# A local-attention transformer on one core: the order of work inside one pipelined step

## Chip, cores and metric

The kernel runs on one core of a Trainium2 chip. Times are device microseconds of one execution. Five engines run their own queues of instructions in order: TensorE (PE, with its weight loads PEld), VectorE (DVE), ScalarE (ACT), GpSimd (POOL) and SyncE (SP), which here only issues DMAs. They wait for one another through semaphores.

## The reference

The input is x, 16 sequences of 256 tokens with 128 channels. Two adaptive layer-norm blocks follow each other. The first has a linear attention and then a six-layer local transformer; the second a causal attention with a position bias and a feed-forward net. The change touches the local transformer alone. Its six layers are, in the reference's words (lines joined and cut):

```python
def attn_layer(x, Wqkv, qs, ksc, Wo):            # 16 heads of 64 channels
    q, k, v = jnp.split(x @ Wqkv, 3, -1)
    q = l2norm(q) * qs;  k = l2norm(k) * ksc
    q = q * cos * scale + rotate_half(q) * sin * scale
    k = k * cos * inv + rotate_half(k) * sin * inv
    out = local_attention(q, k, v)               # windows of 32 queries, 64 keys, softmax
    return out @ Wo
def ffn_layer(x, g, bln, W1, b1, W2, b2):
    hg = layernorm(x) * g + bln;  a, gate = jnp.split(hg @ W1 + b1, 2, -1)
    return a * gelu(gate) @ W2 + b2
for i in range(6):
    x = attn_layer(shift_tokens(x), ...) + x
    x = ffn_layer(shift_tokens(x), ...) + x
```

## The kernel before

All of it is float32, channels on partitions. The 16 sequences form eight units of two sequences (512 tokens). The state of a unit stays on chip as a tile z.

The local transformer is one software-pipelined loop (lines 1002 to 1079) over N = 192 positions: 6 layers x 8 units x 4 steps. A step n starts two head pairs (four of the 16 heads) of a unit, and does later stages of work that began in earlier steps. Inside the block, TensorE, DVE, ScalarE and POOL keep the order in which the source issues instructions (`manual_schedule`, line 991), so the order of the calls in the loop body is the order of each engine's queue. SP is not in that list.

The stages of one pair of steps, with the engines that they use:

- `project` (635): two matmuls per head pair (query and key, line 647) into two PSUM banks; DVE makes from each bank a rotated part `sent` (648) and a straight part (651); ScalarE squares the bank (653). Four DMAs on SP swap halves of `sent` into `got`.
- `rotate` (660): one step later POOL adds `got` to the query and key, four operations of line 662 per step.
- `norms_sum` (665), `norms_inverse` (682), `norms_rows` (719): in every second step the squares of four pairs are summed per head on TensorE (670) and copied by ScalarE to n2 (679), transposed (688), turned to inverse square roots by DVE (690, 699) and eleven small POOL operations (706 to 714), and one step later sent as rows by DMA. `widened` and `scaled` bring the key's factors back and multiply them in on POOL (743).
- `masked` (764) and `scores` (780): four steps after the projection the mask goes into two PSUM tiles `sim`, one for each head of a pair ("par"), and small matmuls (791) add the scores of both pairs ("x").
- `maxima` (800): DVE takes row maxima (803) and makes the Exp's bias nb (805).
- `exponentials` (808): ScalarE runs 16 Exp of 128x64 (812), each followed by a read of its row sum.
- `divided` (821): DVE's reciprocal (823) of all 16 sums and one POOL product (825) over 128x1024.
- `flipped` (829): in the next step TensorE transposes pr (834) into two banks, which ScalarE (842) and DVE (840) copy to prT.
- `windows`, `weighted` (844), `merging` (870): value windows are transposed (753), multiplied by the probabilities (852), copied to zx by ScalarE and DVE (867, 865), and merged with the value-output weights (873) into y. After four steps DVE adds y to the state (886).
- `ffn` (894): the feed-forward of a unit is a generator of ten pieces. `go_on(behind)` is called three times per step and runs one piece at each call. The generator starts at the third call of the step with n = 0 modulo 4 (mean 899, subtraction 901, square 903). At n = 1 the first call does the variance and POOL's power and spreading (917, 919), the third the transposes (924), 925 and 926. At n = 2 the first call does the gates (932, 934), the second the three GELUs (939). At n = 3 the first call does 944 and 948, the third the last matmuls (955) and the addition to the state (888).

PSUM has eight banks: four for the tag "mm" (all products named mm in the profile), three for `sim`, one for y. A tile of "mm" waits until an earlier one has been read for the last time.

The order inside a step before: `scaled`, `rotate`; merging and the addition to the state; norm rows; first `go_on(behind)`; windows; flip; mask; `weighted`; second `go_on`; in even steps the norm sums; scores, maxima, 16 Exp; in even steps the inverse norms; first pair's `project`; third `go_on`; second pair's `project`; `divided`; the row DMAs. ScalarE's queue thus has all 16 Exp ahead of the squares of both pairs.

Of the kernel before, what the change touches and what calls it, by code (L numbers as in the profile page):

```python
# [14 lines left out]
ALU = mybir.AluOpType  # L15
# [29 lines left out]
def adaln_kernel(  # L45
# [5 lines left out]
    nc = tc.nc  # L51
# [27 lines left out]
    def small(tag, shape, bufs=4):  # L79
        return sm.tile(list(shape), F32, tag=tag, name=tag, bufs=bufs)  # L80
# [469 lines left out]
    with ExitStack() as es:  # L550
# [84 lines left out]
        def project(i, u, m, wqk):  # L635


            xs = zs[u][:, :, PAD : PAD + L]
            squares = []
            sent, got = atile("sent", (128, 2, 512)), atile("got", (128, 2, 512))  # L640
            q = two(atile("q", (128, 512), 8))
            k = ks[m % 8][:, :, PAD:]
            for j, (name, r) in enumerate((("q", q), ("k", k))):
                tab = [rope[:, j, a].unsqueeze(1).to_broadcast([128, 2, L]) for a in range(2)]
                scale = bcol(i, name + "s")
                pp = bank()
                nc.tensor.matmul(pp, wqk[:, j, :], xs, start=True, stop=True)  # L647
# [5 lines left out]
                nc.scalar.activation(sq, pp, AF.Square)  # L653
                squares.append(sq)
            for c in range(0, 128, 64):
                nc.sync.dma_start(got[c : c + 32], sent[c + 32 : c + 64])
                nc.sync.dma_start(got[c + 32 : c + 64], sent[c : c + 32])
            return q, squares, got

        def rotate(m, q, got):  # L660
            for j, r in enumerate((q, ks[m % 8][:, :, PAD:])):
                nc.gpsimd.tensor_tensor(r, r, two(got[:, j, :]), ALU.add)  # L662


        def norms_sum(squares):
# [12 lines left out]
            n2 = work("n2")  # L678
            nc.scalar.copy(n2, pn)
            return n2  # L680
# [59 lines left out]
        def scaled(m, kn):  # L740

            k = ks[m % 8][:, :, PAD:]
            nc.gpsimd.tensor_tensor(k, k, two(kn), ALU.mult)  # L743
# [61 lines left out]
            nc.vector.scalar_tensor_tensor(nb, mx, -1.0, rn, ALU.mult, ALU.mult)  # L805
            return nb

        def exponentials(par, sim, nb, rn, pr, ssum):
            for x in range(2):
                for st in range(4):  # L810
                    b = 4 * x + st
                    nc.scalar.activation(  # L812
                        pr[:, x, st, par, :],
                        sim[:, b * 64 : (b + 1) * 64],
                        AF.Exp,
                        bias=nb[:, b : b + 1],
                        scale=rn[:, b : b + 1],
                        accum_out=ssum[:, x, st, par : par + 1],
                    )

        def divided(pr, ssum):
            rsum = small("rsum", (128, 16))
            nc.vector.reciprocal(rsum, ssum.rearrange("p x t h -> p (x t h)"))  # L823
            prf = pr.rearrange("p x t h k -> p (x t h) k")
            nc.gpsimd.tensor_tensor(  # L825
                prf, prf, rsum.unsqueeze(2).to_broadcast([128, 16, 64]), ALU.mult
            )

        def flipped(p, pr, prT):
# [137 lines left out]
        N = DEPTH * per  # L967
        wqk = [load_qk(0, p) for p in range(NP)]
        wff = load_ffn(0)
        vos = {}  # L970
        qs, squares, got, prs, prTs = {}, {}, {}, {}, {}
        xws, zxs, pys = {}, {}, {}
        inverses, kns = {}, {}
        n2 = rk = home = None
        behind, merges = [], []

        def place(n):

            return n // per, n % per // QS, 2 * (n % QS)
# [21 lines left out]
        n = 0  # L1001
        while n < N + 9 or behind:
            layer, at_ = divmod(n, per)
            if at_ == 12 and 0 < layer < DEPTH:
                wff = load_ffn(layer)

            if 0 <= n - 4 < N:
                for x in range(2):
                    scaled(2 * (n - 4) + x, kns.pop(2 * (n - 4) + x))
            if 0 <= n - 1 < N:  # L1010
                for x in range(2):
                    m = 2 * (n - 1) + x
                    rotate(m, qs[m], got.pop(m))

            w, j = divmod(n - 9, QS)
            if 0 <= w < DEPTH * NU:
                if j == 0:
                    pys[w] = psy.tile([128, 512], F32, tag="y", name="y")
                merging(j, zxs.pop((w, j)), vos[w // NU], pys[w])
                if j == QS - 1:  # L1020
                    add_to_state(w % NU, pys.pop(w))
            if n % 2 and 3 <= n <= N + 1:
                home = norms_rows(rk)
            go_on(behind)
            go_on(merges)
            for s, lag in ((0, 7), (1, 9)):
                v, r = divmod(n - lag, QS)
                if r == 0 and 0 <= v < DEPTH * NU:
                    xws[v, s] = windows(v % NU, s)
            if 0 <= n - 5 < N:  # L1030
                i, u, p = place(n - 5)
                if p == 0:
                    prTs[i, u] = atile("prT", (128, NP, 512))
                flipped(p, prs.pop(n - 5), prTs[i, u])
            sims = masked() if 0 <= n - 4 < N else None

            v, r = divmod(n - 8, QS)
            if 0 <= v < DEPTH * NU:
                zxs[v, r] = weighted(r, xws[v, r // 2], prTs[v // NU, v % NU])
            go_on(behind)  # L1040
            if n % 2 == 0 and 2 <= n <= N:
                n2 = norms_sum([squares.pop(m) for m in range(2 * n - 4, 2 * n)])
            if sims:
                m = 2 * (n - 4)
                rn = inverses[m // 4][:, m % 4 // 2]
                scores(sims, m, [qs.pop(m), qs.pop(m + 1)])
                pr = atile("pr", (128, 2, 4, 2, 64), 1)
                ssum = small("ssum", (128, 2, 4, 2))
# [51 lines left out]
    with ExitStack() as es:  # L1100
# [23 lines left out]
        for p in range(NP):  # L1124
            bias = wc.tile([128, 2, 384], F32, tag=f"bias{p}", name=f"bias{p}")
# [176 lines left out]
        N = len(steps)  # L1302
# [3 lines left out]
        qs, prs, prTs, oTs, pys, running, merging = {}, {}, {}, {}, {}, [], []  # L1306
        n = 0
# [147 lines left out]
```

## Time and profile before

| | |
|---|---|
| median of 3 runs | 4600.04 us (4599.63 to 4603.97) |
| the profiled execution's own time | 4603.96 us |
| its span, first to last instruction | 4602.2 us |
| mean granted TensorE clock | 0.966 of full speed |
| busy: PE, PEld | 4075.4 us (89%), 2645.1 us (57%) |
| busy: DVE, ACT, POOL | 2730.6 (59%), 2932.2 (64%), 2572.2 us (56%) |
| busy PE in 440 to 3900 us, the local transformer | 3123.3 of 3460 us, clock 0.99 |

The time of an instruction group, and the idle time of its engine just before it with what ended that idle time, stand in one line of the profile: "busy, mean ns of one | idle us <-releaser". A row of the timeline gives the start and the time taken in us, the engine, the line, the operation and the tiles; a bracket at its end gives the idle time before it. A matmul of float32 shows as two records. Matmuls overlap, so their times do not add up exactly.

### The profile page before, as it was taken

Reading aid. Unit: us, or ns where it says so; the run is one execution under the profiler, and the core shown is the slowest. Engines: PE = TensorE matmul, PEld = TensorE weight load, DVE = VectorE, ACT = ScalarE, POOL = GpSimd, SP = SyncE. Lnnn points to the kernel's source line nnn. Section 1 sums busy time; section 2 is a strip of 40 time slices with the busy share of each in tenths; the row PEclk is TensorE's granted clock in tenths of the full one; section 3 lists DMA queues with packets and bytes.
Section 4 is the critical chain, followed back from the end, with each engine's and each line's share of the span. In section 5 each row is a group of like instructions: output and inputs, shape, how many; then the busy total and the mean of one; then the engine's idle time right before and its main releaser. Section 6 shows DMA issues by size and latency. Waiting matters only on the chain.

```text
span 4602.2 us, 119189 instructions
## 1 busy us (share of the span) xinstructions
PE 4075.4 (89%) x45721; PEld 2645.1 (57%) x45721; DVE 2730.6 (59%) x5795; ACT 2932.2 (64%) x9846; POOL 2572.2 (56%) x3110
## 2 busy tenths in 40 slices
PE   6677799999999989999999999999999998899998
PEld 4443566666666666666666666666665666545454
DVE  3434666666666666666666666666666665455554
ACT  2333666766666676666666666666767666377776
POOL 3323666666666666666666666666665665144332
PEclk8678899999999999999999999999999999899999
DMA  1023444344444344444344344343434432200000
GB/s 30 5 35 91 106 99 100 97 104 100 98 102 103 96 100 102 102 99 102 96 100 105 95 104 100 100 100 94 107 98 100 100 92 73 66 3 3 6 3 8
DMA packets 193553, 371.11 MB, mean 81 GB/s; under 512 B 42537, under 2 KB 83416, under 8 KB 192984
## 3 DMA queue, kind: packets, MB, share of 16 engines
q1 hardware_dynamic: 192984, 363.50, 32.3%
q8 instruction: 361, 5.91, 0.5%
q14 instruction: 208, 1.70, 0.1%
HBM read 127.92 MB, written 8.91 MB: 30 GB/s over the span
## 4 chain that ended last, share of the span: by engine, by line
PE 55%; DVE 19%; ACT 10%; issue 4%; POOL 1%; DMA 0%; DVEq 0%; SPq 0%; POOLq 0%; ACTq 0%
PE y L873 11%; PE mm L852 8%; PE mm L647 6%; PE sim L791 5%; DVE sent L648 5%; PE mm L834 3%; PE mm L944 3%; DVE mx L803 3%; PE mm L932 3%; ACT pr L812 2%; PE mm L955 2%; DVE k L651 2%; PE mm L670 2%; DVE q L651 2%; ACT fg L939 2%
## 5 line engine op out<-in xcount | busy, mean ns | idle before, releaser
L812 ACT ACTIVATE pr<-sim,nb,rq 128x64 f32<-128x64 f32 x3072 | 1190.9, 429 | 283.0 <-DVE nb L805 213.5
L647 PE MATMUL mm<-z,wqk 128*128 128x512 f32 x1536 | 764.0, 611 | 161.2 <-DVE fx L901 63.6
L825 POOL TENSOR_TENSOR pr<-pr,rsum 128x1024 f32<-128x1024 f32 x192 | 365.0, 1901 | 921.9 <-DVE rsum L823 914.1
L873 PEld LDWEIGHTS y<-zx,wvo 128*128 128x128 f32 x6144 | 723.2, 193 | 92.5 <-issue 90.5
L873 PE MATMUL y<-zx,wvo 128*128 128x128 f32 x6144 | 724.4, 277 | 0.8 <-ACT zx L867 0.7
L812 ACT ACTIVATION_READ_ACCUMULATOR pr<-sim,nb,rq 128x1 f32 x3072 | 707.7, 230 | 0.0
L648 DVE SCALAR_TENSOR_TENSOR sent<-mm,vec,rope 128x512 f32<-128x512 f32 x768 | 572.0, 745 | 36.9 <-PE mm L647 28.5
L647 PEld LDWEIGHTS mm<-z,wqk 128*128 128x128 f32 x1536 | 263.6, 191 | 474.2 <-issue 154.2
L662 POOL TENSOR_TENSOR q<-q,got 128x512 f32<-128x512 f32 x384 | 488.2, 1271 | 11.1 <-DMA got<-sent 10.8
L743 POOL TENSOR_TENSOR k<-k,kn 128x512 f32<-128x512 f32 x384 | 480.2, 1271 | 15.7 <-DMA kn<-rkh 15.6
L662 POOL TENSOR_TENSOR k<-k,got 128x512 f32<-128x512 f32 x384 | 488.7, 1273 | 0.0
L803 DVE TENSOR_REDUCE mx<-sim 128x8 f32<-128x512 f32 x384 | 263.8, 687 | 329.2 <-PE sim L791 329.2
L653 ACT ACTIVATE sq<-mm 128x512 f32<-128x512 f32 x768 | 422.8, 672 | 36.9 <-DVE q L651 24.3
L867 ACT COPY zx<-mm 128x512 f32<-128x512 f32 x384 | 224.9, 586 | 347.5 <-PE mm L852 347.5
L852 PE MATMUL mm<-prT,xw 64*128 64x256 f32 x3072 | 391.0, 393 | 24.9 <-DVE prT L840 24.8
L865 DVE COPY zx<-mm 128x512 f32<-128x512 f32 x384 | 265.5, 691 | 227.2 <-PE mm L852 227.2
L1215 POOL TENSOR_TENSOR pr<-pr,rsum 128x256 f32<-128x256 f32 (+1 forms) x256 | 206.1, 826 | 317.6 <-DVE rsum L1213 310.2
L852 PEld LDWEIGHTS mm<-prT,xw 64*128 64x128 f32 x3072 | 294.7, 189 | 131.0 <-ACT prT L842 104.2
L791 PEld LDWEIGHTS sim<-k,q 64*32 64x32 f32 x24576 | 264.9, 105 | 120.8 <-issue 111.3
L791 PE MATMUL sim<-k,q 64*32 64x64 f32 x24576 | 297.7, 226 | 6.4 <-POOL k L743 5.1
L840 DVE COPY prT<-mm 128x512 f32<-128x512 f32 x192 | 132.8, 692 | 270.4 <-PE mm L834 269.2
L1204 ACT ACTIVATE pr<-lg,nm 128x128 f32<-128x128 f32 (+1 forms) x512 | 226.5, 444 | 93.3 <-DVE nm L1193 81.4
(237 smaller groups left out, 6664.1 us busy)
## 6 DMA issues: line engine op xcount, KB each, us to landing
got<-sent SPq DMA_DIRECT2D x1536, 128.0 KB
kn<-rkh SPq DMA_DIRECT2D x768, 128.0 KB
xw<-xw SPq DMA_DIRECT2D x96, 256.0 KB
wqk<-in_L_ffn_Wqkv_dram SPq DMA_DIRECT2D x48, 128.0 KB
bhome<-brow SPq DMA_DIRECT2D x1, 3072.0 KB
wv<-in_L_ffn_Wqkv_dram SPq DMA_DIRECT2D x12, 256.0 KB
wo<-in_L_ffn_Wo_dram SPq DMA_DIRECT2D x12, 256.0 KB
xt<-in_x_dram SPq DMA_DIRECT2D x8, 256.0 KB
```

Source lines behind the costliest of these rows:

```text
L647: nc.tensor.matmul(pp, wqk[:, j, :], xs, start=True, stop=True)
L648: nc.vector.scalar_tensor_tensor(two(sent[:, j, :]), two(pp), scale, tab[1], ALU.mult, ALU.mult)
L653: nc.scalar.activation(sq, pp, AF.Square)
L662: nc.gpsimd.tensor_tensor(r, r, two(got[:, j, :]), ALU.add)
L743: nc.gpsimd.tensor_tensor(k, k, two(kn), ALU.mult)
L791: nc.tensor.matmul(sims[par][32 * c : 32 * c + 32, c0 : c0 + 64], q[r, s, t0 : t0 + 32], k[r, s, t0 : t0 + 64], start=False, stop=True, sk ...
L803: nc.vector.tensor_reduce(mx, sim.rearrange("p (b k) -> p b k", b=8), AX.X, ALU.max)
L812: nc.scalar.activation(pr[:, x, st, par, :], sim[:, b * 64 : (b + 1) * 64], AF.Exp, bias=nb[:, b : b + 1], scale=rn[:, b : b + 1], accum_o ...
L825: nc.gpsimd.tensor_tensor(prf, prf, rsum.unsqueeze(2).to_broadcast([128, 16, 64]), ALU.mult)
L852: nc.tensor.matmul(pz[par][:, w * 256 : (w + 1) * 256], xw[r, (2 * k + w) % 8, :], prT[r, :, 64 * k + 32 * w : 64 * k + 32 * w + 32], star ...
L865: nc.vector.tensor_copy(dst, src)
L873: nc.tensor.matmul(py[:, j * 128 : (j + 1) * 128], vo[:, h, :], zx[:, h % 2, h // 2, :], start=(h == 0), stop=(h == 2 * NP - 1), skip_grou ...
```

## The change

Four things move inside the loop body; no arithmetic on the data is added or removed.

1. The exponentials are done by head pair (x) rather than by head of a pair (par): eight Exp for the first pair, then the first pair's projection with its squares, then eight Exp for the second pair, then the second pair's projection. Sums, reciprocal and POOL product are made per pair: two reciprocals of 128x8 and two products of 128x512 take the place of one of 128x16 and one of 128x1024.
2. The third `go_on(behind)`, a feed-forward piece, runs ahead of both projections rather than between them.
3. The norm sums run ahead of `weighted` and of the second `go_on`, rather than after them.
4. `rotate` runs after the first `go_on(behind)` and `go_on(merges)`, rather than right after `scaled`.

```diff
-        def exponentials(par, sim, nb, rn, pr, ssum):
-            for x in range(2):
+        def exponentials(x, sims, nbs, rn, pr):
+
+            ssum = small("ssum", (128, 4, 2))
+            for par in range(2):
                 for st in range(4):
                     b = 4 * x + st
                     nc.scalar.activation(
                         pr[:, x, st, par, :],
-                        sim[:, b * 64 : (b + 1) * 64],
+                        sims[par][:, b * 64 : (b + 1) * 64],
                         AF.Exp,
-                        bias=nb[:, b : b + 1],
-                        scale=rn[:, b : b + 1],
-                        accum_out=ssum[:, x, st, par : par + 1],
+                        bias=nbs[par][:, b : b + 1],
+                        scale=rn[:, par, b : b + 1],
+                        accum_out=ssum[:, st, par : par + 1],
                     )
+            return ssum
 
         def divided(pr, ssum):
-            rsum = small("rsum", (128, 16))
+            rsum = small("rsum", (128, 8))
...
-                prf, prf, rsum.unsqueeze(2).to_broadcast([128, 16, 64]), ALU.mult
+                prf, prf, rsum.unsqueeze(2).to_broadcast([128, 8, 64]), ALU.mult
             )
...
-            if 0 <= n - 1 < N:
-                for x in range(2):
-                    m = 2 * (n - 1) + x
-                    rotate(m, qs[m], got.pop(m))
...
             go_on(behind)
             go_on(merges)
+            if 0 <= n - 1 < N:
+                for m in (2 * (n - 1), 2 * (n - 1) + 1):
+                    rotate(m, qs[m], got.pop(m))
...
+            if n % 2 == 0 and 2 <= n <= N:
+                n2 = norms_sum([squares.pop(m) for m in range(2 * n - 4, 2 * n)])
             v, r = divmod(n - 8, QS)
             if 0 <= v < DEPTH * NU:
                 zxs[v, r] = weighted(r, xws[v, r // 2], prTs[v // NU, v % NU])
             go_on(behind)
-            if n % 2 == 0 and 2 <= n <= N:
-                n2 = norms_sum([squares.pop(m) for m in range(2 * n - 4, 2 * n)])
             if sims:
...
                 nbs = [maxima(sims[par], rn[:, par]) for par in range(2)]
-                for par in range(2):
-                    exponentials(par, sims[par], nbs[par], rn[:, par], pr, ssum)
+                ssum = exponentials(0, sims, nbs, rn, pr)
...
-            if n < N:
-                i, u, p = place(n)
-                m = 2 * n
-                qs[m], squares[m], got[m] = project(i, u, m, wqk[p])
             if 0 <= w < DEPTH * NU and j == QS - 1:
                 behind.append(ffn(w % NU, w // NU, *wff))
             go_on(behind)
-            if n < N:
-                m = 2 * n + 1
-                qs[m], squares[m], got[m] = project(i, u, m, wqk[p + 1])
-            if sims:
-                divided(pr, ssum)
-                prs[n - 4] = pr
+            for x in range(2):
+                if n < N:
+                    i, u, p = place(n)
+                    m = 2 * n + x
+                    qs[m], squares[m], got[m] = project(i, u, m, wqk[p + x])
+                if sims:
+                    divided(pr[:, x], ssum)
+                    if x == 0:
+                        ssum = exponentials(1, sims, nbs, rn, pr)
+                    else:
+                        prs[n - 4] = pr
```

More of the change, by code (lines that the diff above doesn't have):

```diff
@@ L813, in exponentials @@
                         pr[:, x, st, par, :],
-                        sim[:, b * 64 : (b + 1) * 64],
+                        sims[par][:, b * 64 : (b + 1) * 64],
                         AF.Exp,
-                        bias=nb[:, b : b + 1],
-                        scale=rn[:, b : b + 1],
-                        accum_out=ssum[:, x, st, par : par + 1],
+                        bias=nbs[par][:, b : b + 1],
+                        scale=rn[:, par, b : b + 1],
+                        accum_out=ssum[:, st, par : par + 1],
                     )
+            return ssum
         def divided(pr, ssum):
-            rsum = small("rsum", (128, 16))
-            nc.vector.reciprocal(rsum, ssum.rearrange("p x t h -> p (x t h)"))
-            prf = pr.rearrange("p x t h k -> p (x t h) k")
+            rsum = small("rsum", (128, 8))
+            nc.vector.reciprocal(rsum, ssum.rearrange("p t h -> p (t h)"))
+            prf = pr.rearrange("p t h k -> p (t h) k")
             nc.gpsimd.tensor_tensor(
-                prf, prf, rsum.unsqueeze(2).to_broadcast([128, 16, 64]), ALU.mult
+                prf, prf, rsum.unsqueeze(2).to_broadcast([128, 8, 64]), ALU.mult
             )
@@ L1007, in adaln_kernel @@
             if 0 <= n - 4 < N:
-                for x in range(2):
-                    scaled(2 * (n - 4) + x, kns.pop(2 * (n - 4) + x))
-            if 0 <= n - 1 < N:
-                for x in range(2):
-                    m = 2 * (n - 1) + x
-                    rotate(m, qs[m], got.pop(m))
+                for m in (2 * (n - 4), 2 * (n - 4) + 1):
+                    scaled(m, kns.pop(m))
             w, j = divmod(n - 9, QS)
@@ L1047, in adaln_kernel @@
                 pr = atile("pr", (128, 2, 4, 2, 64), 1)
-                ssum = small("ssum", (128, 2, 4, 2))
                 nbs = [maxima(sims[par], rn[:, par]) for par in range(2)]
-                for par in range(2):
-                    exponentials(par, sims[par], nbs[par], rn[:, par], pr, ssum)
+                ssum = exponentials(0, sims, nbs, rn, pr)
             if n % 2 == 0 and 2 <= n <= N:
                 rk, inverses[n // 2 - 1] = norms_inverse(n2)
-            if n < N:
-                i, u, p = place(n)
-                m = 2 * n
-                qs[m], squares[m], got[m] = project(i, u, m, wqk[p])
             if 0 <= w < DEPTH * NU and j == QS - 1:
```

## The prediction

> **What bounds the kernel now.** I read the page first (busy shares, slices, chain that ended last), then the groups by line, then the timeline of single steps, engine by engine. The slices put about 3,500 of the 4,602 us into the local-attention loop, which is all that the diff touches (first Square of line 653 at 411.7 us, last Exp of line 812 at 3,926.8).
>
> ```profile
> PE 4075.4 (89%) x45721; PEld 2645.1 (57%) x45721; DVE 2730.6 (59%) x5795; ACT 2932.2 (64%) x9846; POOL 2572.2 (56%) x3110
> ...
> PE 55%; DVE 19%; ACT 10%; issue 4%; POOL 1%; DMA 0%; DVEq 0%; SPq 0%; POOLq 0%; ACTq 0%
> ```
>
> TensorE is busiest, but the chain leaves it for 45% of the span: it is paced by hand-backs. The groups name them.
>
> ```profile
> L647 PE MATMUL mm<-z,wqk 128*128 128x512 f32 x1536 | 764.0, 611 | 161.2 <-DVE fx L901 63.6 <-DVE fx L925 52.2 <-DVE z L888 37.9
> ...
> L852 PE MATMUL mm<-prT,xw 64*128 64x256 f32 x3072 | 391.0, 393 | 24.9 <-DVE prT L840 24.8
> ...
> L688 PE MATMUL mm<-ident,n 128*128 128x128 f32 x384 | 63.9, 288 | 51.6 <-ACT n L679 50.3 <-issue 1.2
> ...
> L924 PE MATMUL mm<-ident,fs 128*128 128x128 f32 x192 | 31.7, 288 | 29.2 <-POOL fs L919 29.2
> ...
> L722 PE MATMUL mm<-ident,rk 128*32 128x128 f32 x96 | 26.2, 273 | 40.3 <-ACT sq L653 34.2 <-POOL rk L713 6.1
> ```
>
> Each is one gap per four steps (a unit; 48 units). Sorting TensorE's idle time of 1800 to 2400 us by step number n modulo 4 gives, per unit: 1.45 us at n=0 (line 647 waits for 901) and 0.53 (852 for 840); 1.14 at n=1 (647 for 925) and 0.63 (924 for 919); 1.08 at n=2 (688 for 679) and 0.57 (722 for 653); 0.84 at n=3 (647 for 888) and 0.18 (834 for pr). Sum 6.42, times 48 = **308 us**, the most that reordering can win unless TensorE itself gets cheaper.
>
> Two stretches of the timeline show the mechanisms. The first is n=0, the second n=2.
>
> ```profile
> 2050.59 0.67 DVE L901 TENSOR_TENSOR fx<-z,mm 128x512 f32<-128x512 f32 x1
> ...
> 2051.32 1.12 PE L647 MATMUL mm<-z,wqk 128*128 128x512 f32 x2 [1.45 <-DVE fx L901]
> ```
>
> ```profile
> 2006.61 1.28 ACT L939 ACT_TABLE_LOAD   x1
> ...
> 2007.90 1.95 ACT L939 ACTIVATE fg<-fg,vec 128x512 f32<-128x512 f32 x3
> ...
> 2009.75 0.56 ACT L679 COPY n<-mm 128x512 f32<-128x512 f32 x1
> ...
> 2010.33 1.28 ACT L812 ACT_TABLE_LOAD   x1
> 2010.37 0.66 PE L688 MATMUL mm<-ident,n 128*128 128x128 f32 x4 [1.13 <-ACT n L679]
> ```
>
> In the first, five tiles (two projections of the first pair, the feed-forward piece's, two of the second pair) share four "mm" banks. The first pair's banks are held until its squares, which stand behind 16 Exp; so the last projection takes the feed-forward bank, whose DVE reader stands behind the four line 648/651 operations. In the second, the copy n2 stands behind a table load and three GELUs.
>
> **What the Trainium skill says.** "Perfetto Trace Analysis", Identifying the Most-Contended Engine, says a gap that repeats on the engine that should be saturated can mean too little PSUM for the next tile; the gaps of 1.45, 1.14 and 0.84 us before line 647 fit that. "ScalarE: Activation LUTs", What ACT_TABLE_LOAD costs, gives some 1.28 us for the load and 2.66 us per change of table set with a drain; the load above is 1.28 us, and the next Gelu starts 0.01 us later, so I use 1.28. Exp and Square follow each other here without a load (47 loads at line 812, as many as at 939), so squares among the Exp bring none.
>
> **The change, part by part.** I measure from S, the end of a step's scores on TensorE. From the timeline: DVE does two maxima pairs by S+1.72, the first Exp starts at S+1.0, eight Exp take 3.07 us, a pair of squares 1.15, four operations of lines 648/651 2.66, the reciprocal 0.25, and the POOL product starts 0.4 after a reciprocal. A half product, 128x512, isn't in the loop; the like one at line 1215 takes 1.04 us (bounds: half of 1.90, 0.95, and the 1.27 of line 662). TensorE's projections take 0.87 each, the merging 3.6.
>
> *n=0, S to the next flip (line 834).* TensorE: inverse norms, feed-forward mean, four projections, merging, norm rows, line 907, windows. The mean's bank is now read first on DVE (2.2 to 2.9), before the fourth projection asks at some 4.0: the 1.45 gap closes. Against it: ScalarE does Exp 1.0–4.1, the feed-forward square to 4.8, squares 5.95, Exp 9.0, squares 10.15; the windows of the next step need a bank at 9.55 and get one at about 9.7, and the second half of pr is ready at 10.7, when the second flip asks for it at 10.9. Gain 1.45 - 0.2 = **1.25**.
>
> *n=1.* The piece with lines 924 to 926 comes first; its bank is free at 2.4, asked for at 3.3, so 1.14 closes. Rotations (four line 662 operations, 5.0 us) now stand behind lines 917 and 919, so 924 no longer waits: 0.63 closes. The rotations are delayed 1.6 us by these two; their results are first read three steps later. Who waits for the POOL behind them is the pr product, idle 914 us in all before it, so it has the room. Everything needed by the next step's flip (10.6) is there (pr 10.1, squares 9.45). Gain **1.77**.
>
> *n=2, the part that loses.* The norm sums go ahead of the weighted state, so n2 is copied before the GELUs, and the 1.08 gap closes. But the weighted state moves 1.9 us later, and with it the line 867 copies and the GELUs behind them: zx done about S-0.75, load and GELUs to S+2.5, Exp's load to 3.8, Exp 3.85 instead of 2.4. Then Exp to 6.9, squares 8.1, Exp 11.15, squares 12.3 (before 10.65). The reciprocal of the first half waits on DVE for 6.95 with the second pair's four operations behind it (they end 9.9, no one needs them sooner); that of the second waits for 11.2, with line 948 behind it. TensorE is through merging at 8.05 and norm rows at 8.4. Of the three banks that line 944 wants it gets one at once, the next when the last squares begin to release (11.75), the third at 12.3: line 944 ends at 13.2, windows 14.05, flip 14.2. Before, the flip was at 2022.50 against S=2009.24, 13.26. A **loss of 0.95**, the gaps of 1.08 and 0.57 having given way to one of about 2.65.
>
> *n=3.* Line 955 first: DVE waits for it until S+2.75 (1.0 us idle, the four operations of the first pair behind it), adds the state to 4.25, first pair 6.9, reciprocal 7.2, second pair 9.85, reciprocal 10.1, pr's second half 11.4. TensorE, without the 0.84, could flip at 9.7; its second flip waits to 11.4 and ends at 11.85, against 12.1. Gain 0.25. In the next step the norm sums lie between the flip and line 852, so 0.53 closes: together **0.8**.
>
> Nothing else has a price: the second half's Exp needs no new wait (both nb are there at 1.72); one more reciprocal (0.25) and one more product start per step lie on DVE and POOL, both some 63% busy between 440 and 3,900 us; the line 656/657 DMAs on SP follow their senders by at most 2.4 us at n=2 and are read a step later.
>
> **Sum.** 1.25 + 1.77 - 0.95 + 0.8 = 2.87 us per unit. With the first and last units not full, 47.5: 136 us. The profiled execution took 4,603.96 (span 4,602.2, 1.8 outside it): 4,468. The median of the runs is 3.9 lower: 4,464, said as **4,465**, 2.9% less.
>
> **The rivals.**
> *Little is won* (0.20): ScalarE and DVE take over as bound. At n=2 the delay of the last reciprocal (11.45 against 8.72, 2.7) reaches the flip in full, the windows at n=0 wait for ScalarE and half of its gain goes (0.6), n=3 wins only the 0.53: 0.6 + 1.77 - 2.7 + 0.53 = 0.2 per unit if all of it comes, 10 us, 4,590; half of it, 4,527. For it: ScalarE works almost without a pause from S to the next flip. Against: only n=2 has the GELUs.
> *More is won* (0.16): bank and GELU delays don't bind, and most of 6.42 closes: 5.5 x 47.5 = 260, 4,340. For it: another choice of banks at n=2 is possible. Against: four banks, and 12.3 us of ScalarE work.
> *Slower* (0.07): the two halves of pr are kept apart as tile slices only in the source, and the second half's Exp waits for the POOL product of the first. Then its start moves from 5.3 to 8.65 at n=3, and per unit n=3/0/1/2 give -1.3, -0.5, +0.5, -1.55: -2.85, 135 us, 4,735. It decides as soon as the product ends after the squares, which is so in all steps. Against it: the two halves of zx, one tile, are written at once by ScalarE and DVE.
>
> ```profile
> 2005.14 0.58 ACT L867 COPY zx<-mm 128x512 f32<-128x512 f32 x1 [1.30 <-PE mm L852]
> 2005.18 0.69 DVE L865 COPY zx<-mm 128x512 f32<-128x512 f32 x1 [0.84 <-PE mm L852]
> ```
>
> **How the numbers follow.** My case 0.57, own range 4,420 to 4,515 (1 us per unit either way); little 0.20; more 0.16; slower 0.07. Leaving out the far ends of "more" and "little" and the slower case gives 4,375 to 4,550. About 0.2%, 9 us, is what can be told from no change. Faster 0.89 (all but slower and the far end of little), same 0.03, slower 0.08.
>
> **What would show it.** Right: line 647's idle time by 901, 925 and 888 falls from 154 us to under 30; 688 by 679 and 924 by 919 nearly vanish; a new wait of line 944 for line 653 of about 2 us, 48 times; line 834 waits for pr at n=3; Exp starts 3.8 us after the scores at n=2; no more table loads than 47. Wrong: line 812 waiting for POOL; gaps of line 647 by line 653; or n=2 longer than 21.5 us from mask to mask (20.0 now).

## The result, and the profile after

| | before | after |
|---|---|---|
| median | 4601.84 us (4599.63 to 4603.97, 4 runs) | 4633.01 us (4629.50 to 4644.84, 4 runs) |
| ratio to before, 95% interval | | 1.0072 [1.0053, 1.0091] |
| profiled execution, span | 4603.96, 4602.2 us | 4633.54, 4631.8 us |
| mean granted TensorE clock | 0.966 | 0.956 |

The changed kernel is **31 us slower** where 136 us of gain were forecast. The page after, its busy shares and the engines of the chain that ended last:

```profile
PE 4117.4 (89%) x45721; PEld 2657.6 (57%) x45721; DVE 2794.1 (60%) x5987; ACT 2928.0 (63%) x9846; POOL 2604.9 (56%) x3302
...
PE 42%; DVE 19%; ACT 16%; issue 9%; POOL 4%; DMA 1%; SPq 0%; DVEq 0%; POOLq 0%; ACTq 0%
```

TensorE runs the same 45,721 matmuls and is busy 42 us longer: something made them dearer. In the chain its share fell from 55% to 42%, and ScalarE, POOL and "issue" took it. In the lines below, line numbers are up to three higher than before (834 is now 837, 932 is 935, 944 is 947). First the groups after: busy time, mean ns of one, and after the bar the idle time with what ended it.

```profile
L647 PE MATMUL mm<-z,wqk 128*128 128x512 f32 x1536 | 709.0, 600 | 22.6 <-DVE fx L928 13.8 <-DMA wqk<-in_L_ffn_Wqkv_dram 7.5 <-ACT sq L653 0.4
L653 ACT ACTIVATE sq<-mm 128x512 f32<-128x512 f32 x768 | 444.1, 628 | 217.6 <-DVE q L651 115.5 <-DVE k L651 80.5 <-DMA w<-in_L_ffn_W_dram 15.8
...
L837 PE MATMUL mm<-ident,pr 128*128 128x128 f32 x1536 | 220.3, 283 | 103.7 <-POOL pr L828 103.0
...
L947 PE MATMUL mm<-fx,w 128*128 128x512 f32 (+1 forms) x288 | 173.7, 720 | 115.3 <-ACT sq L653 110.4
...
L935 PE MATMUL mm<-fx,w 128*128 128x512 f32 (+1 forms) x288 | 143.9, 611 | 61.8 <-ACT sq L653 60.3 <-DVE fx L929 1.5
...
L805 DVE SCALAR_TENSOR_TENSOR nb<-mx,rq 128x8 f32<-128x8 f32 x384 | 126.3, 329 | 13.3
...
L688 PE MATMUL mm<-ident,n 128*128 128x128 f32 x384 | 63.4, 288 | 0.7 <-ACT n L679 0.7
```

The gaps that the change was to close are closed: line 647 idles 22.6 us instead of 161.2, line 688 0.7 instead of 51.6. Three others stand in their place: 837 waits for pr (103 us), 947 and 935 wait for squares (110 and 60). Behind them stands the second row: ScalarE's squares wait 218 us, mostly for DVE's q and k. Two rows of the kernel before show how these two things stood there:

```profile
L653 ACT ACTIVATE sq<-mm 128x512 f32<-128x512 f32 x768 | 422.8, 672 | 36.9 <-DVE q L651 24.3 <-DVE k L651 6.8 <-PE mm L647 1.6
...
L805 DVE SCALAR_TENSOR_TENSOR nb<-mx,rq 128x8 f32<-128x8 f32 x384 | 70.6, 184 | 13.3
```

The same stretch of 1800 to 2400 us, cut from mask to mask and averaged by n modulo 4, gives the length of each step and, in parentheses, TensorE's idle time in it (us):

| | n=0 | n=1 | n=2 | n=3 | unit |
|---|---|---|---|---|---|
| before | 19.31 (1.98) | 17.39 (1.77) | 20.03 (1.66) | 16.28 (1.06) | 73.01 (6.47) |
| after | 17.52 (0.25) | 17.18 (1.67) | 21.99 (2.53) | 16.99 (1.81) | 73.68 (6.26) |
| change | -1.79 | -0.21 | +1.96 | +0.71 | +0.67 |
| forecast | -1.78 | -1.77 | +0.95 | -0.27 | -2.87 |

The forecast's 0.53 at line 852 lies in the mask-to-mask step n=0 and is counted there. 0.67 x 48 = 32 us, the 31 measured. n=0 came as forecast; n=1 missed by 1.56, n=2 by 1.0, n=3 by 1.0. Length less idle time is the work: 18.37 before and 19.46 after at n=2, within 0.11 in the other three steps. So n=2 has a loss that is no wait.

**n=3 in the timeline** (start, time taken, engine, line; in brackets the idle time before). Scores end at 2050.83.

```profile
2056.61 0.74 DVE L651 SCALAR_TENSOR_TENSOR q<-mm,vec,rope 128x512 f32<-128x512 f32 x1
2057.44 0.60 ACT L653 ACTIVATE sq<-mm 128x512 f32<-128x512 f32 x1 [2.38 <-DVE q L651]
2057.93 0.74 DVE L651 SCALAR_TENSOR_TENSOR k<-mm,vec,rope 128x512 f32<-128x512 f32 x1
2058.76 0.60 ACT L653 ACTIVATE sq<-mm 128x512 f32<-128x512 f32 x1 [0.72 <-DVE k L651]
...
2062.48 0.20 DVE L826 RECIPROCAL rsum<-ssum 128x8 f32<-128x8 f32 x1 [1.11 <-ACT pr L814]
2062.76 1.04 POOL L828 TENSOR_TENSOR pr<-pr,rsum 128x512 f32<-128x512 f32 x1 [2.78 <-DVE rsum L826]
2063.86 0.66 PE L837 MATMUL mm<-ident,pr 128*128 128x128 f32 x4 [2.06 <-POOL pr L828]
```

ScalarE has done eight Exp and idles 2.38 us: each square starts 0.09 us after the last DVE reader of *the same bank* has ended. The second eight Exp stand behind these squares, so the second reciprocal comes at S+11.65 (S is the end of the scores) and the flip's second half at S+13.0. Of 45 such passes this one alone is some 0.75 us late as a whole, for its matmuls of line 958 ended at S+3.52. In the others they ended at S+2.77 (one 2.84); the squares there start at about S+5.9 and S+7.2, the reciprocal at S+10.9, and pr is ready at S+12.2.

**n=1**, from scores to the gates' wait: the maxima's small second operation runs while POOL rotates.

```profile
2011.42 1.27 POOL L662 TENSOR_TENSOR k<-k,got 128x512 f32<-128x512 f32 x1
2011.76 0.94 DVE L805 SCALAR_TENSOR_TENSOR nb<-mx,rq 128x8 f32<-128x8 f32 x1
...
2012.64 1.26 POOL L662 TENSOR_TENSOR q<-q,got 128x512 f32<-128x512 f32 x1
2013.34 0.59 DVE L805 SCALAR_TENSOR_TENSOR nb<-mx,rq 128x8 f32<-128x8 f32 x1
...
2014.57 0.85 DVE L929 TENSOR_SCALAR fx<-fx,vec 128x512 f32<-128x512 f32 x1
```

An nb of eight columns takes 0.94 us and ends (2012.70) with the POOL operation (2012.69); the next ends at 2013.93, POOL's at 2013.90.

**n=2** on TensorE, after its pause:

```profile
2041.54 2.78 PE L947 MATMUL mm<-fx,w 128*128 128x512 f32 x4 [2.46 <-ACT sq L653]
2044.11 1.91 PE L753 MATMUL mm<-ident,z 128*64 128x128 f32 x8
```

In other passes the four records take 1.83 to 1.98 us, and these eight transposes 1.04. The granted clock tells the two kinds of pass apart. Here is the stretch from the pause's end to the next mask in this pass and in the next one (from and to, length, busy time of each engine with its instructions; PEclk is the clock as a share of full speed):

```profile
core 0: us, PE busy (x) PEld busy (x) DVE busy (x) ACT busy (x) POOL busy (x), PEclk, DMA share, GB/s
2041.54:2046.79 5.25, 5.25 (x21) 3.17 (x22) 2.49 (x4) 1.27 (x4) 5.25 (x5) 0.67 0.25 56
2116.15:2119.72 3.57, 3.57 (x21) 2.45 (x22) 2.48 (x4) 1.27 (x4) 3.57 (x4) 1.00 0.37 84
```

The 0.67 is the mean of 3.41 us at 0.5 and the rest at 1.0. Of the 45 passes with this pause in the whole loop, 28 have a stretch at 0.5 of full clock in what follows the pause; the other 17 keep 1.0. From the pause's end to the mask the first take 5.24 to 5.70 us, the second 3.57.

### The profile page after: what moved, and what is told of

It reads as the page before. It is cut to its first block, busy times and chain, and to the rows that moved or that the text cites. A ratio compares the mean times of both kernels' runs of the same rounds, so it can differ in the third digit from the quotient of the medians.

```text
span 4631.8 us, 119576 instructions
## 1 busy us (share of the span) xinstructions
PE 4117.4 (89%) x45721; PEld 2657.6 (57%) x45721; DVE 2794.1 (60%) x5987; ACT 2928.0 (63%) x9846; POOL 2604.9 (56%) x3302
## 4 chain that ended last, share of the span: by engine, by line
PE 42%; DVE 19%; ACT 16%; issue 9%; POOL 4%; DMA 1%; SPq 0%; DVEq 0%; POOLq 0%; ACTq 0%
ACT pr L814 10%; PE mm L855 8%; PE sim L791 6%; DVE sent L648 5%; PE mm L670 4%; DVE mx L803 4%; PE mm L837 4%; ACT sq L653 3%; PE mm L958 3%; PE mm L947 2%; DVE k L651 2%; PE mm L753 2%; DVE nb L805 2%; POOL pr L828 2%; DVE q L651 2%
## 5 line engine op out<-in xcount | busy, mean ns | idle before, releaser
L814 ACT ACTIVATE pr<-sim,nb,rq 128x64 f32<-128x64 f32 x3072 | 1195.3, 419 | 326.3 <-DVE nb L805 308.3
L828 POOL TENSOR_TENSOR pr<-pr,rsum 128x512 f32<-128x512 f32 x384 | 400.3, 1042 | 1040.5 <-DVE rsum L826 944.2
L647 PE MATMUL mm<-z,wqk 128*128 128x512 f32 x1536 | 709.0, 600 | 22.6 <-DVE fx L928 13.8
L814 ACT ACTIVATION_READ_ACCUMULATOR pr<-sim,nb,rq 128x1 f32 x3072 | 678.3, 221 | 0.0
L653 ACT ACTIVATE sq<-mm 128x512 f32<-128x512 f32 x768 | 444.1, 628 | 217.6 <-DVE q L651 115.5
L647 PEld LDWEIGHTS mm<-z,wqk 128*128 128x128 f32 x1536 | 281.8, 191 | 362.1 <-issue 264.1
L837 PE MATMUL mm<-ident,pr 128*128 128x128 f32 x1536 | 220.3, 283 | 103.7 <-POOL pr L828 103.0
```

What stands on the lines that cost most here:

```text
L814: nc.scalar.activation(pr[:, x, st, par, :], sims[par][:, b * 64 : (b + 1) * 64], AF.Exp, bias=nbs[par][:, b : b + 1], scale=rn[:, par, b ...
L828: nc.gpsimd.tensor_tensor(prf, prf, rsum.unsqueeze(2).to_broadcast([128, 8, 64]), ALU.mult)
L837: nc.tensor.transpose(pt[:, st * 128 : (st + 1) * 128], pr[:, x, st].rearrange("p h k -> p (h k)"), ident,)
```

## The experiments

After the result the theory was: order costs nothing by itself; squares bound to DVE's readers (n=3), nb against POOL (n=1), and TensorE at half rate after the pause (n=2) ate the gain. The rivals: one of the four parts is bad as such, or TensorE's own work is the bound. In all, "per step" means the us of n=0/1/2/3 from mask to mask, and a ratio is to the kernel before, with its 95% interval.

**Undoing one part each.** Part 1, the split of the exponentials:

```diff
-                ssum = exponentials(0, sims, nbs, rn, pr)
+                for par in range(2):
+                    exponentials(par, sims[par], nbs[par], rn[:, par], pr, ssum)
...
-            for x in range(2):
...
-                    divided(pr[:, x], ssum)
+                divided(pr, ssum)
```

> The changed kernel with part 1 undone: all 16 Exp ahead of both pairs' squares again, one reciprocal and one POOL product per step; parts 2, 3 and 4 stay. Theory A (three separate causes: squares in the middle of the Exp wait for the DVE readers of their bank; rotations on POOL meet the nb operations of DVE at n=1; the GELUs are late at n=2): the squares find their banks read, so ScalarE loses its 218 us of waits before line 653; the line 935 gap at n=1 falls from 1.33 to about 0.3, line 947 at n=2 stays over 2, pr at n=3 stays about 1.5: 0.6 to 1.2 us per unit, 4,575 to 4,605. Theory B (the moved norm sums with the late GELUs are the whole loss, parts 1, 2 and 4 bring what was forecast): the time rises, or stays within 5 us of 4,633.

4675.77 us, 1.0160 [1.0145, 1.0175]; per step 18.52/16.47/22.47/17.24. The time rose, as theory B said, and theory A's sign was wrong: the split is a gain of 43 us even in the changed kernel. (B's reason, that the moved sums are the whole loss, isn't borne out: see part 3.) With all squares behind 16 Exp the norm transposes at n=2 wait for a bank, 155.7 us in all, against 12.5 in after (and those for POOL):

```profile
L722 PE MATMUL mm<-ident,rk 128*32 128x128 f32 x96 | 26.7, 278 | 155.7 <-ACT sq L653 146.8 <-POOL rk L713 7.5
```

Part 4, `rotate` back behind `scaled`:

```diff
+            if 0 <= n - 1 < N:
+                for x in range(2):
+                    m = 2 * (n - 1) + x
+                    rotate(m, qs[m], got.pop(m))
...
-            if 0 <= n - 1 < N:
-                for m in (2 * (n - 1), 2 * (n - 1) + 1):
-                    rotate(m, qs[m], got.pop(m))
```

> The changed kernel with part 4 undone: rotations right after the scaling again, ahead of line 920 on POOL. Theory A: at n=1 the nb operations take 0.17 us again instead of 0.94 and 0.59, line 929 0.55 instead of 0.85, the chain DVE, squares, second half of Exp, last squares starts 1.2 to 1.5 us earlier, line 935 waits under 0.3 us; line 927 waits for line 922 again, 0.63 us: net 0.5 to 0.8 us per unit, 4,595 to 4,610. Theory B: only the 0.63 comes back, 30 us slower than the changed kernel, 4,663.

4796.96 us, 1.0421 [1.0403, 1.0438]; per step 17.53/20.51/22.05/17.12. Theory A had the sign wrong, theory B the size. Part 2 brings the transposes of line 927 right behind the scores, and POOL, with 5 us of rotations first, has fs ready 3.8 us per unit later than they ask (181.9/48):

```profile
L927 PE MATMUL mm<-ident,fs 128*128 128x128 f32 x192 | 42.6, 362 | 181.9 <-POOL fs L922 181.9
```

So part 4 is what part 2 needs: beside the other parts it gains 164 us, the price of nb beside POOL included.

Part 3, the norm sums back behind the second `go_on`:

```diff
-            if n % 2 == 0 and 2 <= n <= N:
-                n2 = norms_sum([squares.pop(m) for m in range(2 * n - 4, 2 * n)])
...
             go_on(behind)
+            if n % 2 == 0 and 2 <= n <= N:
+                n2 = norms_sum([squares.pop(m) for m in range(2 * n - 4, 2 * n)])
```

> The changed kernel with part 3 undone: norm sums after the weighted state and after the second feed-forward call. Theory A: at n=2 Exp start 2.4 us after the scores instead of 3.85, the wait of line 947 falls from 2.46 to about 1, no stretch at half rate follows it (line 947 mean 610 ns instead of 720, granted clock 1.00 in the loop), line 688's wait of 1.08 and at n=0 line 855's of 0.53 come back: about 0.8 to 1.5 us per unit, 4,560 to 4,595. Theory B: all that was lost comes back and the other parts' gain with it: below 4,530.

4556.33 us, 0.9903 [0.9888, 0.9918]; per step 18.15/17.02/19.61/16.91, just under theory A's range. n=2 gives back 2.4 us: 1.1 at line 688 return, the 2.46 pause falls to 0.43, and the matmuls behind it cost 609 ns instead of 720:

```profile
L947 PE MATMUL mm<-fx,w 128*128 128x512 f32 (+1 forms) x288 | 143.6, 609 | 20.0 <-ACT sq L653 20.0
```

Part 2, the feed-forward piece back between the projections:

```diff
-            go_on(behind)
             for x in range(2):
...
+                if x == 0:
+                    go_on(behind)
```

> The changed kernel with part 2 undone: the feed-forward piece between the two projections again (after the first pair's division and the second pair's Exp in the queues). Theory A: the forecast for part 2 held, so the waits of line 647 for lines 904, 928 and 891 come back, some 3.4 us per unit, though part of them now lies in the time in which the flip would wait for pr anyway: 0.5 to 2 us per unit slower, 4,655 to 4,730. Theory B: 3.4 us per unit slower, 4,790.

4648.28 us, 1.0101 [1.0086, 1.0116]; per step 18.52/18.02/22.75/14.86. This is just under theory A's range. Part 2 wins 1.0 at n=0 and 0.8 at n=1 and loses 2.1 at n=3, where DVE waits for its matmuls (958). Its 0.8 at n=2 is clock: without part 2, 38 of 45 passes were at half clock after the pause (8 of 8 in the stretch of the table), against 28 of 45.

**The three causes, each by itself.** The squares are cut loose from the banks: they read a constant, so norms and all that follows from them are not the reference's.

```diff
-                nc.scalar.activation(sq, pp, AF.Square)
+                nc.scalar.activation(
+                    two(sq), fixed.unsqueeze(1).to_broadcast([128, 2, 256]), AF.Square
+                )
```

> The changed kernel with one difference: ScalarE squares a constant tile in SBUF instead of the projection's PSUM bank, so the norms (and the output) are not the reference's; the number and length of the squares stay. They no longer wait for DVE's two readers of the bank, and the banks are given back by DVE alone. Theory A: line 653 waits for no DVE (196 us of waits go), at n=3 the second eight Exp start right after the first, pr is ready some 1 us earlier and the wait of line 837 falls from 1.75 to about 0.7; at n=1 line 935 and at n=2 line 947 find banks: 1.0 + 1.3 + 2.5 + 1.1 us per unit less, up to 280 us, 4,350 to 4,480. Rival (pr is late at n=3 because of DVE's own queue, not of the squares): line 837 still waits 1.5 us or more.

4381.8 us, 0.9522 [0.9508, 0.9537]; per step 17.18/15.62/19.90/15.76. In its groups the squares wait for nothing, the flip waits about half as long, and line 952 (947 in after) runs at full rate after 0.32 us per unit of pause:

```profile
L656 ACT ACTIVATE sq<-fixed 128x512 f32<-128x512 f32 x768 | 456.8, 672 | 7.9 <-POOL k L565 7.9
...
L842 PE MATMUL mm<-ident,pr 128*128 128x128 f32 x1536 | 219.3, 280 | 57.6 <-POOL pr L833 57.5
...
L952 PE MATMUL mm<-fx,w 128*128 128x512 f32 (+1 forms) x288 | 148.9, 610 | 15.6 <-DVE k L654 8.8 <-DVE q L654 6.8
```

251 us less than after, as theory A had it; at n=3 the flip waits 0.7 us, so its rival is out. The gain is 0.3, 1.6, 2.1 and 1.2 us at n=0 to 3. So n=1 wins all that was forecast for it, although its nb take 0.76 us in the mean, no less than in after (0.72): the causes are not separate. What delays DVE at n=1 reaches TensorE through a bank that a square still holds. The 251 us are an upper bound for the squares' wait: the banks now also come back after DVE alone, one reader fewer.

The rotations of the step n=1 modulo 4 are left out (a quarter of the queries and keys is not rotated):

```diff
-                    rotate(m, qs[m], got.pop(m))
+                    if n % QS == 1:
+                        got.pop(m)
+                    else:
+                        rotate(m, qs[m], got.pop(m))
```

> The changed kernel without the four rotations in steps n=1 modulo 4 (the rotation of those pairs is left out, so the output isn't the reference's). Theory A: without POOL operations beside them the nb operations take 0.17 us and line 929 0.55 at n=1 (in the changed kernel 0.94, 0.59 and 0.85), the DVE, square and Exp chain starts 1.2 to 1.5 us earlier, line 935 waits 0.3 us or less instead of 1.33, line 647's 0.34 for 928 goes: 1.0 to 1.6 us per unit, 4,555 to 4,585. Rival (the squares' place behind DVE alone makes line 935 wait): line 935 still waits 1 us or more, 4,615 or above.

4610.39 us (4587.53 to 4622.17), 1.0019 [1.0007, 1.0031]; per step 17.37/15.77/22.43/16.91. The step itself gave what was expected, 1.41 us, with nb at 194 ns in the mean (329) and line 929 at 546. Line 935's idle time fell from 61.8 to 25.9 us. The total did not come: 23 us instead of 68, since the clock took more at n=2 (line 947 at 812 ns in the mean). The passes at half clock were about as many as in after, 30 of 45 against 28, but in 17 of them it lasted 6.83 us instead of 3.41. In all, from 600 to 3800 us, the clock was at half for 204.8 us against 122.9; by estimate half of the difference is lost, 41 us, about the 45 that are missing.

The pause of 2.46 us is filled with work that no one reads:

```diff
+                if c == 0:
+                    idle = pss.tile([128, 512], F32, tag="sim", name="idle")
+                    for _ in range(9):
+                        nc.tensor.matmul(idle, ident16, maskb.unsqueeze(1).to_broadcast([128, 2, 256]), start=True, stop=True)
```

> The changed kernel with work added: nine mask matmuls of 0.21 us into a spare sim tile that no one reads, between the first and the second matmul group of line 947, where TensorE waits 2.46 us at n=2. Theory C (a long pause of TensorE itself makes the matmuls behind it run at half rate for some 1.7 us, which is what makes n=2 longer than its gap): with the pause down to about 0.5 us lines 947 and 753 take 0.86 and 0.87 us again, step n=2 goes from 22.0 to about 20.9, granted clock from 0.98 to 0.99 or 1.00: 4,575 to 4,595, faster although nothing is taken away. Rival (the slow matmuls have another cause, such as weights or banks): 4,633 or slower.

4602.85 us (4599.25 to 4609.27), 1.0003 [0.9994, 1.0011]: **30 us less than after, by 432 matmuls more**. That is 8 us above theory C's range, but far from the rival's 4,633. After the pause that is left, 0.5 us, none of the 45 passes has the clock at half. n=2 is 21.06 (21.99), though n=0 gave 0.37 of it back (17.89). The first and third groups are 94 and 34 ns cheaper per record than in after (720 and 310):

```profile
L947 PE MATMUL mm<-fx,w 128*128 128x512 f32 (+1 forms) x288 | 148.9, 626 | 28.1 <-ACT sq L653 23.0
L953 PE MATMUL idle<-maskb,ident 128*128 128x512 bf16 x432 | 101.1, 379 | 0.0
L753 PE MATMUL mm<-ident,z 128*64 128x128 f32 x768 | 102.4, 276 | 16.2 <-DVE ve L918 10.6 <-ACT sq L653 3.9 <-ACT xw L760 1.6
```

**Each part only where it wins.** The undone parts said: sums ahead lose at n=2, the piece ahead loses at n=3.

```diff
-            if n % 2 == 0 and 2 <= n <= N:
+            if n % 4 == 0 and 2 <= n <= N:
...
             go_on(behind)
+            if n % 4 == 2 and 2 <= n <= N:
+                n2 = norms_sum([squares.pop(m) for m in range(2 * n - 4, 2 * n)])
...
-            go_on(behind)
+            if n % 4 != 3:
+                go_on(behind)
...
+                if x == 0 and n % 4 == 3:
+                    go_on(behind)
```

> The changed kernel with two of its moves kept only where they were seen to pay: norm sums ahead of the weighted state at n=0 modulo 4 alone (after it and after the GELUs at n=2), and the feed-forward piece ahead of both projections except at n=3, where it is between them again. From the parts undone: n=2 some 19.6 instead of 22.0 (as with the sums undone), n=3 some 15 instead of 17.0 (as with the piece undone), n=0 17.5, n=1 17.1: 69.2 us per unit instead of 73.7, 4,420 to 4,470. Rival (the parts hang together, and the time won at n=3 is waited out in the next steps): 4,530 to 4,560.

4428.41 us, 0.9625 [0.9610, 0.9639]; per step 17.53/17.16/19.77/14.96, as expected. n=2 and n=3 fall by 2.2 and 2.0, (2.22 + 2.03) x 48 = 204 us, as much as 4633 - 4428.

Before with part 1 alone (its diff is that of part 1 in the change):

> The kernel before with part 1 alone: Exp in two halves with the first pair's projection, squares and division between, the feed-forward piece, the norm sums and the rotations where they were. Theory A: the squares in the middle wait for DVE only where DVE is late; with the piece between the projections DVE reads the first pair's banks by S+4.9, about when eight Exp end, so little is lost; the first pair's banks come back 2 us earlier, but line 647 still waits for the piece's bank (1.45, 1.14, 0.84), so little is won: within 25 us of 4,600. Rival (part 1 in itself is what loses): 4,640 or more.

4508.89 us, 0.9803 [0.9789, 0.9818]; per step 19.46/16.84/19.61/14.98. Both were wrong: the split alone wins 92 us. The earlier squares give two banks back sooner, and line 647 idles 81 us, 69 of them for squares, where it idled 161, nearly all for DVE's fx and z:

```profile
L647 PE MATMUL mm<-z,wqk 128*128 128x512 f32 x1536 | 751.9, 608 | 81.4 <-ACT sq L653 69.0 <-DMA wqk<-in_L_ffn_Wqkv_dram 7.1 <-issue 5.2
```

Before with parts 2 and 4:

> The kernel before with parts 2 and 4: the feed-forward piece ahead of both projections and the rotations behind the first call; all 16 Exp together, norm sums where they were. Theory A: the gaps of line 647 close (3.4 us per unit) and line 924's too (0.63); the first pair's banks come back only after 16 Exp, so gaps of lines 722 and 932 before line 653 appear or grow, and pr is late at n=3 by some 2 us: 1 to 2 us per unit won, 4,505 to 4,555. Rival (the piece ahead only moves the bank wait): 4,590 or more.

4587.36 us, 0.9972 [0.9963, 0.9981]; per step 18.65/16.42/19.99/17.07, between the two. It wins at n=0 and n=1, 1.6 in all, and loses 0.8 at n=3, where the flip idles for pr:

```profile
L834 PE MATMUL mm<-ident,pr 128*128 128x128 f32 x1536 | 216.3, 287 | 126.3 <-POOL pr L825 122.9
```

The mixed order without part 1 (the exponentials as before):

> The mixed version without part 1: all 16 Exp together, one division. Shows what part 1 is worth once the other moves sit well. Theory A: without it the first pair's banks come back 2 us later at n=1 and n=2, lines 932 and 944 or 722 wait 0.5 to 1.5 us more in both: 4,460 to 4,530, so part 1 wins 1 to 2% there. Rival (part 1 costs something everywhere by squares that wait for DVE): below 4,428.

4516.00 us, 0.9820 [0.9803, 0.9836]; per step 18.20/16.58/20.08/16.28, as theory A had it. Part 1 is worth 88 us in it.

The mixed order, with the row maxima written to a PSUM tile, so that nb reads only one input from SBUF:

```diff
-            mx = small("mx", (128, 8))
...
-                nbs = [maxima(sims[par], rn[:, par]) for par in range(2)]
+                mx = pss.tile([128, 512], F32, tag="sim", name="mx")
+                nbs = [maxima(sims[par], rn[:, par], mx[:, 8 * par : 8 * par + 8]) for par in range(2)]
```

> The mixed version with the row maxima mx written to a sim tile in PSUM instead of SBUF, so that the nb operation of DVE has one input in SBUF and not two; same arithmetic, same order. Theory A (nb is held up only because two SBUF inputs meet POOL's rotations): nb takes 0.17 to 0.2 us also at n=1, line 935's wait falls from 1.34 to 0.3 to 0.7 us: 0.6 to 1.0 us per unit, 4,380 to 4,405. Rival (nb is long at n=1 for another reason, as its place or its semaphore): nb stays at 0.33 us on average, 4,428 or slower.

**4379.12 us** (4378.11 to 4380.84), 0.9521 [0.9507, 0.9535]; per step 17.57/16.20/19.77/15.00, as theory A had it, within 1 us of its range. n=1 wins 0.96 us x 48 = 46 of the 49 us. Its nb, 332 ns in the mixed order:

```profile
L804 DVE SCALAR_TENSOR_TENSOR nb<-mx,rq 128x8 f32<-128x8 f32 x384 | 64.1, 167 | 13.3
```

Nothing is left out in it, and it is 4.8% faster than the kernel before.

## Why the prediction was wrong

Of its four steps one held and three failed, by 1.56, 1.0 and 1.0 us of a unit, which is 3.5 x 48 = 170 us. The signs that it named for being right all came (the closed gaps, the new waits of 944 for squares and of 834 for pr, the late Exp at n=2), so it had most waits right. The steps that failed put three costs at nothing: POOL's rotations beside DVE's small operations (n=1), a pause that costs more than its length (n=2), and squares that wait for DVE's readers of the same bank (n=3).

- **n=0: right.** Forecast -1.25 and the 0.53 at line 852, measured -1.79. Line 647's waits for 901, 925 and 888, 154 us, fell below 30, as they should if they were for lack of a PSUM bank. (The sentence of "Perfetto Trace Analysis" by which the prediction read them stands under Optimization Strategy, not under the heading that it names.) Here DVE reads the mean's bank and does the first pair early, so the squares hardly wait.
- **n=1: a cost left out.** The step read "the rotations are delayed 1.6 us ...; their results are first read three steps later" and asked only who waits for POOL. It didn't ask which DVE work lies beside POOL at the new place. nb (0.17 where nothing runs beside it) took 0.94 and 0.59, and line 929 0.85 instead of 0.55; the chain behind them, DVE's readers, squares and the bank, ends in line 935's 1.33 us. "SBUF — State Buffer", Who interferes with whom, in the Trainium skill says it outright: a DVE instruction with two SBUF inputs contends with a GpSimd instruction that reads SBUF, over a port pair held as an exclusive lock. The trace agrees: all 138 nb of after that took over 0.3 us end within 0.05 us of a rotation on POOL, and with one input in PSUM nb is back at 167 ns. Without the rotations n=1 gains 1.41 of the missing 1.56; with mx in PSUM 0.96, and 0.89 at the gates (42.7/48) stays. With the squares off the bank all 1.56 comes, nb as long as before: the link that failed is nb's delay together with the held bank, not nb alone.
- **n=2: the gap right, the clock not foreseen.** The prediction had one gap of about 2.65 at line 944 and a loss of 0.95; the gap was 2.46, and where the clock stayed full the step took 20.93, a loss of 0.90. But after the gap TensorE was at half clock in 5 of 9 passes: from the gap's end to the next mask mostly 5.25 us, against 3.57 in the other four. 1.68 x 5/9 = 0.93, nearly all of the missing 1.0 (in the whole loop 1.68 x 28/45 = 1.05). Filling the pause gave 0.93 of n=2 back. The prediction's own sign of being wrong here, n=2 above 21.5 us, came true.
- **n=3: the wrong resource.** "Adds the state to 4.25, first pair 6.9, ... second pair 9.85" had DVE right (4.33, 7.09 and 9.79 in nearly all passes), but the 16 Exp and four squares on ScalarE were taken to run on without a wait ("squares 5.95" at n=0, and the like here). A square runs only when DVE's two operations on that bank are done, so at S+5.9 and S+7.2; the last reciprocal, which DVE was free for at 9.79, came at 10.9 rather than 10.1, and the second half of pr at S+12.2 rather than 11.4. The wait of line 834 was forecast; its size, 1.75 us in the mean and 2.06 in most passes, was not (by the forecast's numbers 0.6: asked for at 12.1 - 0.84 - 0.45 = 10.8, ready at 11.4; measured 10.2 and 12.2). The row of before had hinted at it: 31 of the 36.9 us that the squares idled were DVE's q and k. It was small because 16 Exp stood ahead of the squares; the split leaves eight, and part 2 at the same time puts DVE behind the matmuls of line 958 and the addition to the state. Cut loose from the bank, pr is ready at S+11.0, and the wait falls to 57.5/48 = 1.2 us per unit in all, 0.7 of it at n=3. The split is not the culprit: without it, but with the piece ahead, the flip waits 1.97 us, there because one reciprocal stands behind all of DVE's eight projection operations. The piece ahead makes DVE late; the split only changes the way by which that reaches pr.
- **The rivals.** None named what happened. "Little is won" was nearest, with ScalarE and DVE as the bound, but it put the loss at n=2 and gave 4,527 to 4,590. "Slower" needed the Exp of the second half to wait for POOL's product; line 814 shows no such wait (308.3 of 326.3 us idle are for nb).
- **Where the gain went.** The four parts are not additive. Alone, the split wins 92 us and the piece with the rotations 13; in the mixed order, with the two losing places taken back, all reach 173. The two places cost 204 together: the sums ahead at n=2 (a 1.1 us gap closed for a 2.46 us gap that also slows what follows), and the piece ahead at n=3 (a 0.84 us gap closed, DVE's reading of the first pair delayed, and with it squares, Exp, pr and flip).

Open stays how the 251 us of the squares' experiment divide between the wait and the banks' earlier return. Why some passes at n=2 were slow and others not, the trace of after does show. Its granted clock is 1.0 or 0.5 and changes on a raster of 3.41 us. In the 28 slow passes at least 1.98 us of the pause lay within one interval of the raster, in the 17 others at most 1.93; so the same pause is dear or cheap by where it falls. The limit is not as sharp everywhere: without the rotations of n=1, half clock followed from 1.49 us on in some passes.

## What to carry to other kernels

Before work is moved ahead on one engine, follow the moved buffer's other readers: a reader that seemed free of waits may only have been covered by the work that is now behind it, and its row in the profile (36.9 us idle, by DVE) says so. A reorder in a periodic loop is best judged per phase of the period: the same edit won 1 us at n=0 and lost 2 at n=3, and applying it by phase turned 4633 us into 4428. When an engine is moved beside another, look at the small operations there too; here a 0.17 us operation set 46 us of the kernel. And a pause has a price beyond its length where the clock falls behind it.

## What the runs showed of the hardware

- **A short pause can halve TensorE's clock.** After 2.46 us the granted clock fell to 0.5 in 28 of 45 passes of the changed kernel and in 38 of 45 without part 2, mostly for 3.41 us; after some 2.0 us (n=1 without part 2) in 4 of 8 (9.63 against 7.98 us for the same stretch); in the kernel before after 1.0 to 1.6 us never, in 22 pauses, and after 1.93 us in all five. Eight transposes took 1.91 us instead of 1.04. "TensorE: Matmul & The Clock Gate", HAM oscillation, in the Trainium skill, gives as its rule that there be no gaps above about 3.4 us; here shorter ones cost 1.68 us each, and the measurement decides. Nine matmuls for nothing in each pause saved 30 us.
- **A tiny DVE operation can be held to the end of POOL's**: nb of 128x8 took 0.94 us beside a 128x512 POOL sum of 1.27 us and ended with it, 0.17 alone.
- A product 128x512 with a broadcast factor took POOL 1.04 us, a sum of two full tiles 1.27.
